# Two graph layers: weight bursts of seven pairs, the turned u of layer 1 on ScalarE, and numerators set apart

## The chip, the cores and the metric

The kernel runs on one core of one Trainium2 chip. The metric is the device time in microseconds; lower is better. A kernel's time is the median of several executions. One execution is recorded by the hardware profiler, and all durations below come from that one.

## The reference

Two graph layers, each with a residual and a layer norm, on x of 8 batches, 2048 nodes and 64 features, with a dense adjacency matrix A of 2048 x 2048:

```python
def layernorm(x): ...                       # over the 64 features

# layer 0: supports I, A, 2AA - I
x_g = einsum('knm,bmc->bnkc', [I, A, 2*A@A - I], x)
w   = einsum('nd,dkio->nkio', embedding, weight)      # weights of every node, d = 16
x   = layernorm(x + einsum('bnki,nkio->bno', x_g, w) + embedding @ bias)

# layer 1: supports I, A, 2AA - I, softmax(relu(E @ E.T))
apt = softmax(relu(E @ E.T), axis=1)
x_g = einsum('knm,bmc->bknc', [I, A, 2*A@A - I, apt], x)
w   = einsum('nd,dkio->nkio', E, weights_pool)
x   = layernorm(x + einsum('bnki,nkio->bno', x_g, w) + E @ bias_pool)
```

All is in float32. Every node has weights of its own, made from its 16-number embedding.

## The kernel before, in words

The nodes are cut into 8 blocks of 256 (j). The work is 40 stages, one after the other: A0 (u = A x, layer 0), B0 (A u), A1 (u = A x, layer 1), Z1 (softmax times x), V1 (A u), each for j = 0 to 7; stage n is 8 times the phase plus j. `A0` and `A1` are the "u stages". Most stages form their product by Strassen's seven half-size products (`strassen`, `times`): seven accumulations of 8 steps, 56 steps in all. A step in A0 and A1 is one matmul of 128 x 128 by 128 x 256, which the profile lists as two rows. The other stages have 64 steps.

Around the steps of a product the rest of the work is laid by hand. `put(n, place, job)` books a job in stage n at a place from 0 to 64; a stage of 56 steps scales it by 56/64. `catch_up` runs after each step whatever is due. All engines keep the program's order (`Pinned`), so the booking is the order of the work on every engine and in every queue.

The jobs that matter here are these.

- `weights` (line 327) makes the weights of the block's 256 nodes: 32 pairs of matmuls (the two of a pair stand in rows 0 to 63 and 64 to 127 of the array), tile name `pw`, from a slice of the weight tensor (`wst`) and the repeated embeddings (`e2`). Before, the unit is a group of two pairs, four matmuls, in one `ps_big` tile of two PSUM banks: each row half has a bank of its own. Three groups are made in a burst, since there are three such tiles; a stage has 16 groups in bursts of 3, 3, 3, 3, 2, 2. Each group is read out to `w` by ScalarE, some by VectorE, as 128 x 1024.
- The weights of stage n are made in stage n + 1, where also its `turn` (the transposes `pt` of u), its `apply` (64 matmuls `po`, 128 rows of the profile) and `post` stand.
- `wst` is an `Ahead` queue of three tiles of eight pairs each. A stage needs four slices, 0 to 3, loaded by SP's DMA queue (512 KB each). A tile is loaded again once the matmuls that read it are over. Before, the queue is filled when the next slice is taken, and at the end of a stage.
- `adj`, another such queue of four tiles on SP's DMA queue, brings the pieces of A or their sums, one for each of the seven products.
- The accumulators `ps_acc` are two single banks used in turn, one for each of the seven products; the three `ps_big` tiles have the other six banks.
- `store_c` stores the softmax's row maxima and inverse sums (`cd`) by POOL's queue, in each A1 stage; `store_u` stores u of A1 by SP's.
- `numerators` and `normalize` make the softmax's numerators for stage 25 in stage 24, on PE, VectorE and ScalarE.

The loading queue, as it was:

```python
def next(self):
    self.fill()
    return self.ready.pop(0)
```

Of the kernel before, what the change touches and what calls it, by code (L numbers as in the profile page):

```python
# [9 lines left out]
F32 = mybir.dt.float32  # L10
F32R = mybir.dt.float32r
AF = mybir.ActivationFunctionType
# [3 lines left out]
P = 128  # L16
N = 2048
B = 8
C = 64
D = 16  # L20
NJ = N // P
BC = B * C
NB = 256
# [6 lines left out]
V1 = C // 4  # L30
# [18 lines left out]
def two_graph_layers(ctx: ExitStack, tc: tile.TileContext, x, x_t, adj_b, adj_q, layers, out):  # L49
# [30 lines left out]
    three = ctx.enter_context(tc.tile_pool(name="three", bufs=3))  # L80
    small = ctx.enter_context(tc.tile_pool(name="small", bufs=2))
    dram = ctx.enter_context(tc.tile_pool(name="dram", bufs=1, space=bass.MemoryType.DRAM))
    ps_acc = ctx.enter_context(tc.tile_pool(name="ps_acc", bufs=2, space=PSUM))
    ps_big = ctx.enter_context(tc.tile_pool(name="ps_big", bufs=3, space=PSUM))

    def heads(t):
        return t.rearrange("p (b c) -> p b c", b=B)

    def big(name):
        return ps_big.tile([P, 2, 512], F32, tag="big", name=name)  # L90

    def copy(i, dst, src):

        if i % 2:
            act.activation(dst, src, AF.Copy)
        else:
            dve.tensor_copy(dst, src)
# [42 lines left out]
    ps = big("pi")  # L140
# [87 lines left out]
    class Ahead:  # L228
# [10 lines left out]
                self.load(t, self.order.pop(0))  # L239
                self.ready.append(t)  # L240

        def next(self):
            self.fill()
            return self.ready.pop(0)

    def load_adj(t, key):
# [26 lines left out]
    class Stage:  # L273
# [50 lines left out]
                pool.dma_start(out=rows, in_=heads(bx))  # L324


        def weights(self, g0, g1):
            if g0 == 0:
                self.w = w_room[:, 0:NB * self.units].rearrange("p (n o) -> p n o", n=NB)
            made = []  # L330
            for g in range(g0, g1):
                if g % 4 == 0:
                    self.ws = wst.next()
                ps = big("pw").rearrange("p h (v n) -> p h v n", n=NB)
                for i in range(2):
                    for h in range(2):
                        r = slice(64 * h, 64 * h + 64)
                        pe.matmul(ps[:, h, i, :], self.ws[r, 2 * (g % 4) + i, :], self.e2[r, :],
                                  start=True, stop=True)
                made.append(ps)  # L340
            if g1 == self.units // 4:
                wst.fill()
            for g, ps in zip(range(g0, g1), made):
                dst = self.w[:, :, 4 * g:4 * g + 4].rearrange("p n (v h) -> p n v h", h=2)
                copy(0 if self.n and g % (8 if self.phase == "A0" else 3) == (2 if self.phase == "A0" else 1) else 1, dst, ps.rearrange("p h v n -> p n v h"))


        def apply(self, c):
# [65 lines left out]
        def turn(self, k, feature=None):  # L414
            slabs = X[SB * self.j:SB * self.j + SB] if feature == "x" else self.slabs
            order = list(range(SB) if feature == "x" or self.phase == "A0" else reversed(range(SB)))
            ps = big("pt")
            psv = ps.rearrange("p a (q n) -> p (a q) n", n=P)
            for s in order:
                for q in range(BQ):  # L420
                    pe.transpose(psv[:, s * BQ + q, :], slabs[s][:, q * P:(q + 1) * P], ident)
            t = self.features()
            for s in order:
                for par in range(2):
                    src = psv[64 * par:64 * par + 64, s * BQ:(s + 1) * BQ, :]
                    copy(s, t[64 * k:64 * k + 64, s * P:(s + 1) * P, par::2], src.rearrange("p q n -> p n q"))


        def product(self):
# [26 lines left out]
                yield [a[:, i, :] for i in range(4)]  # L456

        def accumulator(self, name):
            return ps_acc.tile([P, BC], F32, tag="acc", name=name)

        def straight(self, right):
            accs = [self.accumulator("pu") for _ in range(SB)]
# [331 lines left out]
    def put(n, i, f, *args):  # L794
        plans[n].setdefault(i * stages[n].length / 64, []).append((f, args))

    def spread(n, first, last, jobs):
        for i, job in enumerate(jobs):
            put(n, first + (last - first) * i / max(len(jobs) - 1, 1), *job)
# [25 lines left out]
        put(32, place, sums["V1"].make, i)  # L825
    for n, st in enumerate(stages):
        phase = st.phase
        cuts = (0, 3, 6, 9, 12, 14, 16) if st.units == C else (0, 3, 6, 8)
        if phase == "V1" and st.j:
            put(n, 4, st.weights, 0, 1)  # L830
            cuts = (1, 4, 7, 10, 13, 16)
        weights = [(st.weights, *g) for g in zip(cuts, cuts[1:])]
        bursts = None
        if phase == "A0":
            for c in range(NJ // 4 if st.j == 1 else 0):
                put(n, 16 * c + 10, st.sums_of_a, c)
            spread(n + 1, 1, 31, weights)
            turned, bursts, posts = 33, (38, 38, 38, 38), (50,)
        elif phase == "B0":
            for c in range(NJ // 4 if st.j == 0 else 0):  # L840
                put(n, (10, 26, 36, 57)[c], st.sums_of_a, c)
            if st.j == 7:
                spread(n, 35, 54, weights)
                bursts, posts = (0, 0, 6, 10), ()
                put(n + 1, 16, st.load_x, range(SB))
                for k in range(6):
                    put(n + 1, (11 if k < 3 else 12.5) + 0.5 * k, st.post, k % 3, 8 - k // 3 * 8, 16 - k // 3 * 8)
            else:
                spread(n + 1, 3, 13, weights)
                bursts, posts = (19, 19, 29, 29), (38, 46.5, 50)  # L850
                put(n + 2, 5, st.load_x, range(SB))
        elif phase == "A1":
            spread(n + 1, 12, 34.5, weights)
            turned, bursts, posts = 4, (43, 43, 43, 43), (56,)
            for s, h, place in ((0, 0, 38), (0, 1, 40), (1, 0, 57), (1, 1, 60)):
                put(*((n, place) if st.j or s == 0 else (n + 1, place - 43)), st.scores_of_rows, s, h)
            put(n, 41, st.statistics, 0)
            put(*((n, 62) if st.j else (n + 1, 19)), st.statistics, 1)
            put(n + 1, 24, st.store_c)
        elif phase == "V1":  # L860
            spread(n, (22 if 0 < st.j < 7 else 12 if st.j else 4), (62 if st.j < 7 else 42), weights)
            bursts, posts = (4, 4, 4, 4), (15, 19, 23)
            put(n, 20, st.load_z)
        if bursts and n + 1 < len(stages):
            if phase[0] == "A":
                put(n + 1, turned, st.turn, 1)
            for i, place in enumerate(bursts):
                put(n + 1, place, st.apply, i if phase == "A0" else i ^ 2)
            for k, place in enumerate(posts):
                put(n + 1, place, st.post, k)  # L870
        if n + 1 < len(stages):
            if n < 24 or n > 30:
                put(n, 44 if n < 23 else 37 if n < 24 else 4, stages[n + 1].load_e)
        if phase[0] == "A":
            put(n, 48 if n == 0 else 36 if st.li == 0 else 38.5, st.bias)
            if st.li == 0:
                put(max(n, 1), 20 if n else 4, st.load_xt)
            else:
                put(n, 47 if st.j else 57, st.turn, 0, "x")
        if phase != "Z1":  # L880
            put(*((1, 26) if n == 0 else (n, 54) if st.kk == 0 else (n, 30)), st.load_acc)
        elif st.narrow:
            put(24, 1, st.take_halves)
            put(23, 48, st.load_e)
            for t, places in enumerate(((3, 5, 37), (7, 10, 40))):
                for i, place in enumerate(places):
                    put(24, place, *((st.numerators, t, i) if i < 2 else (st.normalize, t)))
            put(26, 10, load_last_phase)
        elif st.wide:
            first, even, odd = (n - 2, (16, 24, 32), (40, 48, 56)) if n % 2 == 0 else (n - 2, (28, 36, 44), (4, 12, 20))  # L890
            load = ((25, 40) if n == 28 else (n - 3, 4)) if n % 2 == 0 else (n - 3, 10)
            if n == 26:
                first, even, odd, load = 25, (4, 12, 18), (22, 30, 36), (24, 40)
            elif n == 27:
                first, even, odd, load = 25, (66, 69, 72), (44, 52, 58), (25, 8)
            put(*load, st.load_e)
            for t, places in enumerate((even, odd)):
                for i, place in enumerate(places):
                    at = (first, place) if place < 64 else (first + 1, place - 64)
                    put(*at, *((st.numerators, t, i) if i < 2 else (st.normalize, t)))  # L900
        else:
            st.p = [None] * 8
            for c in range(8):
                if c < 3:
                    put(n - 1, (50, 54, 62)[c], st.scores, c)
                else:
                    put(n, 8 * (c - 2), st.scores, c)
# [73 lines left out]
```

## Time and profile before

| What | Value |
|---|---|
| median of 3 runs | 1468.82 us (1468.38 to 1470.13) |
| profiled execution | 1470.19 us |
| its span, first to last instruction | 1468.3 us |
| TensorE busy | 1440.8 us, 98% of the span |
| VectorE busy | 973.9 us, 66% |
| ScalarE busy | 478.3 us, 33% |
| GpSimd busy | 204.6 us, 14% |
| matmuls `pw` | 1728 (wst) and 64 (first stage), 146.5 and 5.3 us busy |
| read-outs of `pw` | 330 on ScalarE at 1.02 us, 118 on VectorE at 1.22 us |
| loads of `wst` | 108 of 512 KB, median 6.1 us from issue to landing |
| granted TensorE clock | 0.998 of full speed |

Busy is the time in which an engine has an instruction at work, and instructions of one engine can overlap. The profile's groups give, after a bar, the idle time of the engine just before the group's instructions and what ended it. The chain of waits is followed back from the last instruction, and shows at each place what the end hung on. In the timelines and the chain the first number is the start in us, the second the duration, and "x12" the count of rows merged.

### The profile page before, as it was taken

The numbers are of one execution on the slowest core, as the hardware profiler recorded it, in microseconds if no ns is written. First come the engines' busy times: TensorE is split into PE (matmuls) and PEld (weight loads), VectorE is DVE, ScalarE is ACT, GpSimd is POOL, SyncE is SP. The second block draws the span as 40 slices with busy tenths as digits, with TensorE's granted clock in tenths as the row PEclk, the third lists the DMA queues.
The fourth block names the chain that finished last, engine by engine and source line by source line (L and its number), as shares of the span: only waits on it lengthen the run. The fifth ranks groups of instructions, "written<-read, shape, count | busy, mean of one in ns | idle before, by whom it ended". The sixth has DMA issues, their size and how long they took to land.

```text
span 1468.3 us, 31599 instructions
## 1 busy us (share of the span) xinstructions
PE 1440.8 (98%) x13502; PEld 1184.9 (81%) x13502; DVE 973.9 (66%) x1655; ACT 478.3 (33%) x597; POOL 204.6 (14%) x339
## 2 busy tenths in 40 slices
PE   9999999999999999999999999999999999999996
PEld 4577777778999999567777777799888988888885
DVE  3866666648676766865666666679794666666666
ACT  0444444432211213154444344612110233333332
POOL 4212221110111111211011111011000000000000
PEclk9999999999999999999999999999999999999999
DMA  9888888886666666578887977223313766666662
GB/s 361 274 262 276 282 280 265 281 313 190 209 192 201 205 201 206 157 177 180 205 201 162 207 205 186 35 73 101 90 44 105 236 196 190 189 194 191 190 206 59
DMA packets 88380, 285.50 MB, mean 194 GB/s; under 512 B 14000, under 2 KB 19632, under 8 KB 86640
## 3 DMA queue, kind: packets, MB, share of 16 engines
q1 hardware_dynamic: 55568, 175.13, 41.0%
q0 software_dynamic: 27200, 94.71, 21.4%
q10 hardware_dynamic: 5472, 13.63, 2.8%
q8 instruction: 107, 1.75, 0.5%
q14 instruction: 33, 0.27, 0.1%
HBM read 217.33 MB, written 62.41 MB: 191 GB/s over the span
## 4 chain that ended last, share of the span: by engine, by line
PE 91%; DVE 4%; DMA 3%; ACT 1%; issue 1%; ACTq 0%; DVEq 0%
PE p L43 58%; PE po L43 14%; PE pw L43 9%; PE pu L43 4%; PE pz L43 4%; DMA wst<-wd 2%; PE pt L43 1%; PE pr L43 1%; PE ps L43 1%; DVE acc L43 1%; DMA x<-in_x 1%; DVE u L43 1%; DVE t L43 0%; DVE p L43 0%; ACT t L43 0%
## 5 line engine op out<-in xcount | busy, mean ns | idle before, releaser
L43 ACT ACTIVATE w<-pw 128x1024 f32<-128x1024 f32 x330 | 320.1, 1021 | 444.4 <-PE pw L43 442.6
L43 DVE SCALAR_TENSOR_TENSOR acc<-po,mask,acc 128x256 f32<-128x256 f32 (+1 forms) x640 | 247.1, 426 | 66.8 <-PE po L43 56.5
L43 DVE COPY w<-pw 128x1024 f32<-128x1024 f32 x118 | 144.4, 1224 | 142.3 <-PE pw L43 142.1
L43 PE MATMUL p<-a,u 128*128 128x128 f32 x1920 | 234.1, 278 | 0.6 <-issue 0.6
L43 PEld LDWEIGHTS p<-a,u 128*128 128x128 f32 x1920 | 221.2, 192 | 8.8 <-issue 2.4
L43 PE MATMUL po<-w,t 128*32 128x256 f32 (+1 forms) x5120 | 206.9, 337 | 7.0 <-issue 5.8
L43 PE MATMUL p<-u,a 128*128 128x256 f32 x832 | 204.3, 388 | 0.0
L43 PEld LDWEIGHTS po<-w,t 128*32 128x32 f32 (+1 forms) x5120 | 128.3, 108 | 79.3 <-issue 16.3
L43 PEld LDWEIGHTS p<-u,a 128*128 128x128 f32 x832 | 151.6, 190 | 29.2 <-issue 5.4
L43 PE MATMUL p<-x,a 128*128 128x256 f32 x624 | 152.4, 384 | 0.0
L43 PE MATMUL pw<-e,wst 64*128 64x256 f32 x1728 | 146.5, 297 | 4.3 <-DMA wst<-wd 2.5
L43 PEld LDWEIGHTS pw<-e,wst 64*128 64x128 f32 x1728 | 112.5, 184 | 46.0 <-issue 23.9
L43 PEld LDWEIGHTS p<-x,a 128*128 128x128 f32 x624 | 114.7, 190 | 19.3 <-issue 0.5
L43 PE MATMUL p<-a,x 128*128 128x128 f32 x768 | 93.0, 277 | 0.0
L43 PEld LDWEIGHTS p<-a,x 128*128 128x128 f32 x768 | 88.3, 192 | 2.5 <-PE pw L43 0.2
L43 PE MATMUL pu<-x,a 128*128 128x512 f32 x192 | 87.0, 600 | 2.1 <-DMA x<-in_x 2.1
L43 PE MATMUL p<-w,u 128*128 128x256 f32 x384 | 85.8, 379 | 0.0
L43 PE MATMUL p<-a,w 128*128 128x128 f32 x672 | 81.3, 277 | 0.0
L43 PEld LDWEIGHTS p<-w,u 128*128 128x128 f32 x384 | 72.0, 190 | 9.3
L43 PEld LDWEIGHTS p<-a,w 128*128 128x128 f32 x672 | 77.3, 192 | 2.5 <-issue 1.4
L43 PEld LDWEIGHTS pu<-x,a 128*128 128x128 f32 x192 | 35.1, 190 | 42.7 <-issue 37.1
L43 DVE TENSOR_TENSOR temps<-p,temps 128x256 f32<-128x256 f32 x115 | 45.8, 420 | 34.1 <-PE p L43 33.3
(129 smaller groups left out, 1372.7 us busy)
## 6 DMA issues: line engine op xcount, KB each, us to landing
wst<-wd SPq DMA_DIRECT2D x108, 512.0 KB, 6.1
a<-in_adj_q SPq DMA_DIRECT2D x90, 512.0 KB, 5.3
a<-sd SPq DMA_DIRECT2D x88, 512.0 KB, 4.6
sd<-a POOLq DMA_DIRECT2D x24, 512.0 KB, 6.3
bx<-bx POOLq DMA_DIRECT2D x32, 256.0 KB, 5.9
acc<-bx POOLq DMA_DIRECT2D x16, 512.0 KB, 7.1
pd<-acc POOLq DMA_DIRECT2D x16, 512.0 KB, 5.3
acc<-pd POOLq DMA_DIRECT2D x16, 512.0 KB, 8.7
```

Of the source, the lines that this page charges most:

```text
L43: return self._tc.keep_in_program_order(f(*args, **kwargs))
```

## The change

Twelve stage products (n = 1 to 6 and 17 to 22, so A0 and A1 with j = 1 to 6) have their weights made in bursts of 4, 7, 7, 7 and 7 pairs, where there were six bursts of 6, 6, 6, 6, 4 and 4. Six pairs of a burst of seven stand in the three big tiles as before. The seventh, the last by number, stands in the accumulator bank that is not in use. As both of its row halves then write to one bank, they are put at the two ends of the burst: the half in the lower rows is the burst's first matmul, that in the upper rows its last. A one-element activation on ScalarE ("seen") reads the first one's result, and the last matmul waits for it. The spare bank is read out by ScalarE as 128 x 512, after the first big tile.

The places of these bursts are listed by hand. The weight queue is filled after each burst, not ahead of taking a slice, and counts the slice still in use. Which groups VectorE reads out is chosen anew. In layer 1, the copies out of the turned u are all ScalarE's, where VectorE had half. For stage 25 the numerators of the second half and both normalizations change places.

The diff's core:

```diff
-    ps_acc = ctx.enter_context(tc.tile_pool(name="ps_acc", bufs=2, space=PSUM))
+    ps_acc = ctx.enter_context(tc.tile_pool(name="ps_acc", bufs=1, space=PSUM))
...
+    in_use = [0]
+    in_turn = mybir.DependencyInfo(mybir.DependencyClass.Sync, mybir.DependencyReason.DATA)
+
+    def acc_bank(i):
+
+        return ps_acc.tile([P, BC], F32, tag=f"acc{in_use[0] ^ i}", name="pa")
...
-        def next(self):
-            self.fill()
+        def next(self, fill=True):
+            if fill or not self.ready:
+                self.fill()
             return self.ready.pop(0)
...
-        def weights(self, g0, g1):
-            if g0 == 0:
+
+        def weights(self, v0, v1):
+            if v0 == 0:
                 self.w = w_room[:, 0:NB * self.units].rearrange("p (n o) -> p n o", n=NB)
...
+                self.ws = {}
+            for c in range(v0 // 8, (v1 - 1) // 8 + 1):
+                if c not in self.ws:
+                    self.ws[c] = wst.next(fill=False)
+            pairs = list(range(v0, v1))
+            made = [(v, big("pw").rearrange("p h (v n) -> p h v n", n=NB)) for v in pairs[:-1:2]]
+            spare = []
+            if len(pairs) % 2:
+                spare = [pairs.pop()]
+                made.append((spare[0], acc_bank(1).rearrange("p (h v n) -> p h v n", h=2, n=NB)))
+            for at in zip(spare + pairs, pairs + spare):
+                for h, v in enumerate(at):
+                    r = slice(64 * h, 64 * h + 64)
+                    i, ps = (v - v0) % 2, made[(v - v0) // 2][1]
+                    ins = pe.matmul(ps[:, h, i, :], self.ws[v // 8][r, v % 8, :], self.e2[r, :], start=True, stop=True)
+
+                    if v in spare and not h:
+                        seen = act.activation(small.tile([1, 1], F32, tag="seen", name="seen"), ps[0:1, h, i, 0:1], AF.Copy)
+                    elif v in spare:
+                        tc.add_manual_dep(ins.ins, seen.ins.name, in_turn, reason="one bank, two row tiles")
+            wst.held = 1 if v1 % 8 else 0
+            wst.fill()
+            if spare:
+                made.insert(1, made.pop())
+            for k, (v, ps) in enumerate(made):
+                m = 1 if v in spare else 2
+                dst = self.w[:, :, 2 * v:2 * v + 2 * m].rearrange("p n (v h) -> p n v h", h=2)
+                on_dve = k == (0 if self.phase == "V1" else len(made) // 2) and v not in spare and self.n and (v > 16 if self.phase == "A0" else self.phase != "V1" or v0)
+                copy(0 if on_dve else 1, dst, ps.rearrange("p h v n -> p n v h"))
...
-                    copy(s, t[64 * k:64 * k + 64, s * P:(s + 1) * P, par::2], src.rearrange("p q n -> p n q"))
+                    copy(1 if self.phase == "A1" and feature is None else s, t[64 * k:64 * k + 64, s * P:(s + 1) * P, par::2], src.rearrange("p q n -> p n q"))
...
-            return ps_acc.tile([P, BC], F32, tag="acc", name=name)
+            in_use[0] ^= 1
+            return acc_bank(0)
...
+        sevens = n in (*range(1, 7), *range(17, 23))
+        cuts = (0, 2, 8, 14, 20, 26, 32) if phase == "V1" and st.j else (0, 6, 12, 16) if st.half else (0, 4, 11, 18, 25, 32) if sevens else (0, 6, 12, 18, 24, 28, 32)
         weights = [(st.weights, *g) for g in zip(cuts, cuts[1:])]
...
         if phase == "A0":
...
-            spread(n + 1, 1, 31, weights)
-            turned, bursts, posts = 33, (38, 38, 38, 38), (50,)
+            if sevens:
+                place_weights(n + 1, (1, 5, 14, 23, 32))
+                turned, bursts, posts = 34.5, (39.5, 39.5, 39.5, 39.5), (51,)
+            else:
+                spread(n + 1, 1, 31, weights)
+                turned, bursts, posts = 33, (38, 38, 38, 38), (50,)
...
         elif phase == "A1":
-            spread(n + 1, 12, 34.5, weights)
+            if sevens:
+                place_weights(n + 1, (1, 12.5, 17, 22.3, 31.3))
+            else:
+                spread(n + 1, 12, 34.5, weights)
...
-            for t, places in enumerate(((3, 5, 37), (7, 10, 40))):
+            for t, places in enumerate(((3, 7, 22), (37, 39.5, 57))):
```

More of the change, by code (lines that the diff above doesn't have):

```diff
@@ L324, in bias @@
                 pool.dma_start(out=rows, in_=heads(bx))
-        def weights(self, g0, g1):
-            if g0 == 0:
+        def weights(self, v0, v1):
+            if v0 == 0:
                 self.w = w_room[:, 0:NB * self.units].rearrange("p (n o) -> p n o", n=NB)
[L330 to L345, printed above, removed]
+                self.ws = {}
[26 more added lines that the diff above has]
+                copy(0 if on_dve else 1, dst, ps.rearrange("p h v n -> p n v h"))
@@ L827, in two_graph_layers, with place_weights @@
         phase = st.phase
[L828 to L831, printed above, removed]
+        sevens = n in (*range(1, 7), *range(17, 23))
+        cuts = (0, 2, 8, 14, 20, 26, 32) if phase == "V1" and st.j else (0, 6, 12, 16) if st.half else (0, 4, 11, 18, 25, 32) if sevens else (0, 6, 12, 18, 24, 28, 32)
         weights = [(st.weights, *g) for g in zip(cuts, cuts[1:])]
+        def place_weights(n, places):
+            for place, job in zip(places, weights):
+                put(n, place, *job)
         bursts = None
@@ L860, in two_graph_layers @@
         elif phase == "V1":
+            if st.j:
+                put(n, 4, *weights.pop(0))
             spread(n, (22 if 0 < st.j < 7 else 12 if st.j else 4), (62 if st.j < 7 else 42), weights)
```

## The prediction

> **What bounds the kernel now.** I read the page's busy times first.
>
> ```profile
> PE 1440.8 (98%) x13502; PEld 1184.9 (81%) x13502; DVE 973.9 (66%) x1655; ACT 478.3 (33%) x597; POOL 204.6 (14%) x339
> ```
>
> TensorE (PE) is busy in all but 27.5 us of the 1468.3 us span. So a change pays only by shortening PE's own work, and costs what it makes PE wait. ScalarE has room on average. The groups by shape show the weight matmuls and their waits:
>
> ```profile
> L43 PE MATMUL pw<-e,wst 64*128 64x256 f32 x1728 | 146.5, 297 | 4.3 <-DMA wst<-wd 2.5 <-DVE p L43 0.7 <-DVE sq L43 0.5
> L43 ACT ACTIVATE w<-pw 128x1024 f32<-128x1024 f32 x330 | 320.1, 1021 | 444.4 <-PE pw L43 442.6
> ```
>
> To price a burst I took PE's timeline of one stage A0 (start us, us, instruction, count):
>
> ```profile
> 116.62 0.97 PE L43 MATMUL pw<-e,wst 64*128 64x256 f32 x12
> 117.53 2.86 PE L43 MATMUL p<-x,a 128*128 128x256 f32 x12
> 120.31 0.97 PE L43 MATMUL pw<-e,wst 64*128 64x256 f32 x12
> ...
> 130.09 0.74 PE L43 MATMUL pw<-e,wst 64*128 64x256 f32 x8
> 130.76 0.92 PE L43 MATMUL p<-u,a 128*128 128x256 f32 x3
> ```
>
> Start to start, a burst of 12 takes 0.91 us and one of 8 takes 0.67: 0.06 each and 0.19 fixed. The 12 product matmuls after the first burst take 2.78 us; undisturbed ones take 6.14/28 = 0.219 us each (a run of 28 from 106.50 to 112.64), or 2.63. That is 0.15 more. **A burst costs 0.34 us whatever its size.** A step of the product is two such rows, 0.438 us.
>
> Then the chain of waits in one stage A1, which starts at 752.55 (first burst less 11 steps and 0.87 us of transposes, 5.69 us):
>
> ```profile
> 758.31 0.91 PE pw L43 x12
> 759.22 1.92 PE p L43 x8
> 761.14 0.48 PE pw L43 x5
> 761.62 8.57 DMA wst<-wd
> 770.19 0.14 issue
> 770.32 0.74 PE pw L43 x8
> ```
>
> This is the line that decides. The stage's last slice of weights (wst, slice 3) is asked for when burst 2 frees a buffer (761.62) and lands 8.57 us later, just when burst 5 needs it (PE waits 0.68 us). The other A1 stages are alike: issued 9.06 us after the stage's start, landed 17.18, 16.41, 17.64, 17.76, not recorded, and 17.77 us after it. It is late not because it is asked for late. The same stretch of the next-earlier stage (starting at 711.17), by windows (us, busy ..., PEclk, DMA share, GB/s):
>
> ```profile
> 714.00:723.00 9.00, 9.00 (x62) 7.14 (x62) 3.83 (x4) 5.98 (x10) 0.00 (x0) 1.00 0.64 60
> 723.00:728.00 5.00, 5.00 (x38) 3.94 (x34) 3.21 (x6) 3.88 (x4) 0.72 (x1) 1.00 1.02 357
> ```
>
> For 9 us the DMA engines report themselves 64% busy and move 60 GB/s; then the backlog drains at 357. Each of the sixteen small stores cd (1 KB each, two per A1 stage, one issued at 711.86) is followed by such a stretch. Ahead of slice 3 on SP's queue stand the stores of u (0.5 MB) and two loads of adjacency (1 MB), so it comes out after them.
>
> **What the Trainium skill says.** TensorEngine Tiling (Key Properties): changing the tiling mode drains the TensorE. The trace agrees; the 0.34 us are that price. The same page (Gotcha 1: PSUM Pressure): different row tiles cannot access one PSUM bank at once. The trace before shows no such pair, as each half has its own bank; the change needs a handshake for it. DMA: Bandwidth & Descriptors (Queues, rings and completion order): on each engine descriptors are consumed in ring order. The landings agree: adjacency issued at 754.39 and 757.05 landed at 766.38 and 767.65, the slice of 761.62 after them. TensorE: Matmul & The Clock Gate (What's actually happening): an idle window of about 3.4 us halves the clock. PE's longest gap inside the work here is 1.34 us, so only the kernel's end shows it (0.72 of the clock at 1460 to 1464 us).
>
> **The change part by part.**
>
> *Bursts of seven.* Twelve stage products (six A0, six A1) have five bursts, of 8, 14, 14, 14, 14 matmuls, for six. The matmul count stays. A0: 6 x 0.34 = -2.0 us. A1: also -2.0.
>
> *The handshake.* The spare pair's first matmul is followed by a one-element read on ScalarE ("seen"), and the burst's last matmul waits for it. A matmul lasts 0.28, ScalarE starts 0.09 after a finished group (as at 717.41), and the ScalarE rows of 512 and 256 elements (0.60, 0.375) extrapolate to 0.16 for one: 0.6 us, against 13 x 0.06 = 0.8 until the last matmul. Nothing, if ScalarE is free. In A0 it has per burst at most 0.2 + 3 x 0.96 + 0.55 + 0.39 (a product's copy) = 4.0 us between bursts 4.7 apart; so it is, narrowly. The spare is read out second and needed three steps (1.3 us) after the burst; I find some 0.2 us to spare. Bounds 0 and 0.5 us for each of A0's two tightest bursts, 0 to 6 us; I take +0.5. A0's slice 3 is needed 8.7 us after its issue; there it lands in 4.5 to 5.3 us. No wait.
>
> *The earlier need in A1.* The seventh pair of burst 4 is pair 24, of slice 3, and its matmul is the burst's first. Burst 4 stands at step 20: 20 x 0.438 + 0.87 (transposes) + 0.82 (burst of 8) + 2 x 1.18 (bursts of 14) = **12.8 us after the stage's start**, against 17.0 for burst 5 before. The load is issued at about 6.7 us instead of 9.06, yet behind the same stores, loads and slow stretch; the small store that starts the latter hangs on the end of the preceding stage, which the change leaves. So it lands where it did, at 16.4 to 17.8. Waits: 4.4, 3.6, 4.8, 5.0, 4.1 (the landing not recorded taken as 16.9) and 5.0 = 26.8 us. The waits of before, 2.5, are in that. Net **+24.3**; with the bursts saved, A1 gives +22.3. Behind the waiting matmul stands all of PE's order. An earlier issue could gain at most its own 2.4 us; I take 0.
>
> *Turned u on ScalarE, A1 alone.* Sixteen copies leave VectorE (0.69 us each) for ScalarE (0.64). At a stage's start ScalarE then has two exponentials and their reads (to 2.9 us), one eviction (0.96), four copies (2.5) and a product's copy (0.37): done at 6.9, while burst 2 wants that product's bank at 6.5. A wait of 0.45; burst 3 ends one step before a product that takes the bank of its spare, another 0.7. Both lie ahead of slice 3's landing, which swallows them: 0. Without that cover they cost 6 x 1.2 = 7 us.
>
> *Numerators apart.* In stage 24 (Z1, j=0) PE waits 1.34 us (scores) and 0.75 us (weights) behind VectorE, whose queue holds both halves' numerators and the turned u at once. The second half moves to places 37, 39.5 and 57, and the copies go: -2.1. Bounds -2.1 and +1, if three score tiles in a row held up the apply matmuls at place 43.
>
> *The rest.* Weight loads filled after each burst, three more VectorE evictions (121 for 118), other pairs chosen for them, and banks by name: SP's order shifts only by a slice ahead of an adjacency load, with no wait where PE stands. Zero, cover: PE's weight queue three tiles deep; -1 to +2.
>
> Sum: -2.0 + 0.5 + 22.3 - 2.1 = +18.7 us. The profiled execution took 1470.19 us (span 1468.3 and 1.9 around it), 1.37 above the median of the runs, 1468.82. So 1488.9 as profiled, **1487.5** as a median.
>
> **The rivals.**
>
> *The slice comes in time* (faster). Weight loads have a median of 6.1 us to landing; issued at 6.7 us, slice 3 would then be there at 12.8, just at burst 4. This decides if the slow stretch is not bound to the small stores but to what PE or the evictions do, and moves with them. Then A1 gives -2.0 - 2.5 and up to +7 of ScalarE's waits, and the total is between -8.1 and -0.9; at the middle 1464.3. Against it: sixteen small stores, sixteen slow stretches, and other stages, with the same evictions, load in 4.5 to 6.
>
> *The wait also costs clock.* Gaps of 3.6 to 5.0 us reach the skill's window. If each brings one window of 3.4 us at half speed, 1.7 us is lost in six stages, 10 us more: 1497.7. For it the length; against it that the window runs free and may not fit into so short a gap.
>
> *The bursts save nothing* because the shared bank stalls each one: 24 A0 bursts with up to 0.3 us give +7 for the +0.5, 1494. ScalarE's margin there is thin.
>
> **How the numbers follow.** About 0.2%, 2.9 us, is what a measurement of this kernel can tell from no change. Forecast 0.72, clock lost 0.09, banks stalling 0.06: all slower; the slice in time 0.13, split 0.10 faster and 0.03 within. The forecast's own range is 1480 (an earlier issue gaining 1 us a stage) to 1491. The low end lies a little below that, the high end takes in most of the clock case: 1474 to 1497.
>
> **What would show it.** In the changed kernel: PE's wait for DMA wst rises from 2.5 us to about 27, in six gaps some 42 to 46 us apart in A1, each before the first matmul of burst 4; the A0 period shrinks from 38.7 to about 38.4; the two waits of stage 24 are gone; PE's busy time falls by about 4 us. I am wrong if slice 3 lands under 13 us after its stage's start, if A1's stages don't grow by 3 to 5 us, or if PE waits for "seen" in A0.

## The result, and the profile after

The change makes the kernel slower by 22.0 us: 1490.63 us (median of 4 runs, 1488.82 to 1493.45) against 1468.60 before (the three runs above and a fourth), ratio 1.0151 with a 95% interval of 1.0139 to 1.0163. The prediction said 1487.5, in a range of 1474 to 1497. The profiled execution took 1490.48 us, its span is 1488.6, which is 20.3 us more than the span before: the profiled execution before was 1.6 us slower than the median. The terms below are read from the profiles, so they add up to 20.3.

The page after, its busy times and the chain by line:

```profile
PE 1441.8 (97%) x13502; PEld 1187.5 (80%) x13502; DVE 967.1 (65%) x1642; ACT 496.4 (33%) x682; POOL 204.1 (14%) x339
...
PE pa L43 65%; PE po L43 13%; PE pw L43 7%; DMA wst<-wd 4%; PE pt L43 1%; DVE acc L43 1%; PE ps L43 1%; PE pr L43 1%; DMA x<-in_x 1%; DVE u L43 1%; DMA a<-in_adj_q 0%; DVE mean L43 0%; DMA sd<-sums 0%; ACT w L43 0%; DVE w L43 0%
```

PE is busy for almost the same time (1441.8 against 1440.8 us); the span has grown around it. Accumulators are now named pa, and so are the two matmuls of a burst's spare pair, which write to the same banks. What PE waited for (us in total, times, longest):

```profile
PE pa L43 <- DMA wst<-wd: 15.1, 6, 4.0
...
PE pa L43 <- ACT w L43: 3.4, 6, 0.6
PE pa L43 <- ACT temps L43: 2.7, 6, 0.5
...
PE pa L43 <- ACT seen L43: 0.3, 1, 0.3
```

Three waits, six times each: the slice of weights, and two of ScalarE's. The handshake ("seen") shows once, at 0.3 us. The six are the A1 stages with bursts of seven; the chain of waits in one of them, which starts at 757.7 (the stage starts are worked out from the first apply matmul ahead of them, to some 0.1 us):

```profile
764.38 0.38 ACT temps L43
764.76 0.04 issue
764.80 0.38 PE pa L43
765.18 0.48 PE pw L43 x10
765.66 8.30 DMA wst<-wd
773.96 0.14 issue
774.10 0.35 PE pa L43
```

First ScalarE's copy of a product, which burst 2 waits for; then slice 3, asked for 8.0 us after the stage's start and landed 16.3 after it; then, at once, burst 4's first matmul. The same stretch by windows (us, busy PE, PEld, DVE, ACT, POOL, then PEclk, DMA share, GB/s):

```profile
766.00:769.00 3.00, 3.00 (x23) 2.38 (x23) 1.28 (x2) 2.66 (x5) 0.00 (x0) 1.00 0.51 35
769.00:774.20 5.20, 2.54 (x12) 1.61 (x12) 0.84 (x1) 2.14 (x4) 0.00 (x0) 1.00 0.97 375
```

The slow stretch of before is still there, 35 GB/s, and the queue then drains at 375 with PE idle for half of the time. In A0 the bursts themselves take what was forecast. PE's timeline:

```profile
119.05 0.39 PE L43 MATMUL pa<-e,wst 64*128 64x256 f32 x1
119.06 1.09 PE L43 MATMUL pw<-e,wst 64*128 64x256 f32 x12
119.87 0.27 PE L43 MATMUL pa<-e,wst 64*128 64x256 f32 x1
120.08 1.56 PE L43 MATMUL pa<-x,a 128*128 128x256 f32 x6
```

Fourteen matmuls take 1.03 us (119.05 to 120.08), as 0.19 + 14 x 0.06 says. An A0 stage takes 38.24 us, before 38.72.

By phases, from the first apply matmul of one stage to that of the next: A0 -2.1 us (272.0 for 274.1), B0 +0.8, the six A1 stages +22.8 (273.9 for 251.1), stage 24 -1.55 (47.40 for 48.95), Z1 +0.1, V1 +0.7; the kernel's start -0.5.

### The profile page after: what moved, and what is told of

Its sections match the earlier page's. It is cut to its first block, busy times and chain, and to the rows that moved or that the text cites. A ratio compares the mean times of both kernels' runs of the same rounds, so it can differ in the third digit from the quotient of the medians.

```text
span 1488.6 us, 31613 instructions
## 1 busy us (share of the span) xinstructions
PE 1441.8 (97%) x13502; PEld 1187.5 (80%) x13502; DVE 967.1 (65%) x1642; ACT 496.4 (33%) x682; POOL 204.1 (14%) x339
## 4 chain that ended last, share of the span: by engine, by line
PE 89%; DMA 5%; DVE 4%; issue 1%; ACT 1%; ACTq 0%; SPq 0%; DVEq 0%
PE pa L43 65%; PE po L43 13%; PE pw L43 7%; DMA wst<-wd 4%; PE pt L43 1%; DVE acc L43 1%; PE ps L43 1%; PE pr L43 1%; DMA x<-in_x 1%; DVE u L43 1%; DMA a<-in_adj_q 0%; DVE mean L43 0%; DMA sd<-sums 0%; ACT w L43 0%; DVE w L43 0%
## 5 line engine op out<-in xcount | busy, mean ns | idle before, releaser
L43 PE MATMUL pa<-a,u 128*128 128x128 f32 (+1 forms) x2048 | 264.3, 285 | 2.5 <-issue 2.4
L43 PEld LDWEIGHTS pa<-a,u 128*128 128x128 f32 x2048 | 245.0, 192 | 15.2 <-issue 5.2
L43 PE MATMUL pa<-x,a 128*128 128x256 f32 (+1 forms) x816 | 239.2, 435 | 1.2 <-DMA x<-in_x 1.2
L43 PE MATMUL pa<-u,a 128*128 128x256 f32 x832 | 205.4, 391 | 3.4 <-ACT w L43 3.4
L43 PEld LDWEIGHTS pa<-x,a 128*128 128x128 f32 x816 | 149.7, 190 | 61.5 <-issue 37.6
L43 PEld LDWEIGHTS pa<-u,a 128*128 128x128 f32 x832 | 153.8, 192 | 34.5 <-ACT w L43 5.8
L43 PE MATMUL pa<-a,x 128*128 128x128 f32 x768 | 93.0, 277 | 0.0
L43 PEld LDWEIGHTS pa<-a,x 128*128 128x128 f32 x768 | 88.3, 192 | 2.4
L43 PE MATMUL pa<-w,u 128*128 128x256 f32 x384 | 85.8, 379 | 0.0
L43 PE MATMUL pa<-a,w 128*128 128x128 f32 x672 | 81.3, 277 | 0.0
```

Source lines behind the costliest of these rows:

```text
L43: return self._tc.keep_in_program_order(f(*args, **kwargs))
```

## The experiments

Each ratio is to runs of the kernel before that were made beside the experiment. Their median was 1468.84 us beside e1 to e4, 1466.73 beside e5 to e8 and 1466.46 beside e9 and e10, so across these groups the ratios are compared, not the times.

**Take the bursts of seven away, all or in A1 alone.**

```diff
-        sevens = n in (*range(1, 7), *range(17, 23))
+        sevens = False                # e1
+        sevens = n in range(1, 7)     # e2
```

Expected of e1: 

> No stage has bursts of seven; all else of the change stays (fill after each burst, banks by name, turned u on ScalarE, numerators apart, VectorE's choice of groups). Theory 1 (the early need of slice 3 in A1 is the whole loss): A1's waits for wst fall from 15.1 to about 2.5 us as in the kernel before, the two waits of stage 24 are still gone, so about 1.5 us under the kernel before, 1467. Theory 2 (the loss comes from the fill after each burst or the copies on ScalarE): it stays near 1490, or at least 5 us above the kernel before.

Expected of e2: 

> Bursts of seven in layer 0's six u stages alone; layer 1's are six bursts as before. Theory 1: the saved bursts of A0 come on top of the run without any bursts of seven, about 2 to 2.5 us, so 1464.5 to 1465.5, and no wait for wst in A1 over 2.5 us in all. Theory 2 (the shared bank's handshake stalls each burst, and A1 shows it): A0 gains nothing or loses, 1467 or above.

e1: 1467.92 us, ratio 0.9996 (0.9987 to 1.0005). e2: 1468.17, ratio 0.9999 (0.9991 to 1.0008). Both are back at the kernel before, so the loss hangs on A1's bursts of seven. PE's waits for wst are 2.2 and 0.9 us in all. But A0's gain is not seen in e2's time, which is what its theory 2 said, though the profile has the gain (A0 272.05 us) and shows one wait for the handshake, of 0.3 us. Against e1's profile, what takes it back is B0 (321.1 us for 319.8) and stage 24 (48.83 for 47.40). In the nine profiles with bursts of seven in A0, B0 takes 320.1 to 322.0; in the three without, 319.2 to 319.8. Its own instructions are in the same order. That B0 gives back about 1.2 us is measured. By the traces 1.1 us of it are waits of PE for which the profile names no cause: they sum up to 5.6 to 7.6 us in B0 in the nine profiles and to 4.9 to 5.7 in the three. They are of the kind that e7 shows below; why they are longer was not tested.

**Turn the two small stores round.** The inverse sums, which wait for ScalarE, go ahead of the row maxima in POOL's queue, so that both start well after slice 3 is asked for.

```diff
-            for k, a in enumerate((cst, inv[:, :, 0])):
+            for k, a in ((1, inv[:, :, 0]), (0, cst)):
```

Expected in the changed kernel, e3: 

> The changed kernel with one thing turned round: of store_c's two small stores, the inverse sums go ahead of the row maxima in POOL's queue. The first waits for ScalarE until some 14 us into the stage, so the second, too, starts only after slice 3 is needed. Theory 1 (the small store slows the DMA engines): slice 3 lands 4.5 to 6.5 us after its issue, the wait of 15.1 us before burst 4 is gone or under 2 us, and with it the two drops of the clock (3.8 us); ScalarE's waits in A1 (0.46 and 0.56 us a stage) stay. 1490.6 - 15 - 3.8 = about 1472. Theory 2 (the slow stretch belongs to the store of u or to PE's bursts): slice 3 still lands 16.4 to 17.8 us after the stage's start, 1488 to 1492.

e3: 1472.93 us, ratio 1.0032 (1.002 to 1.0045); some 18 us of the 22 are gone. PE no longer waits for wst at all. Slice 3 of the stage that starts at 710.7, asked for at 718.7:

```profile
L43 SPq DMA_DIRECT2D wst<-wd x1: 320/320/320, 718.7 to 718.7; - x1
...
DMA to landing us min/median/max: 3.3/3.3/3.3
```

In the six stages it lands 3.3 to 4.2 us after its issue, 11.3 to 12.2 after the stage's start; in the change 7.7 to 10.2 after the issue, 15.7 to 18.2 after the start. In the stage that starts at 710.7 the two stores are now issued at 727.9 and 728.6. The same columns by windows:

```profile
719.00:727.00 8.00, 7.42 (x51) 5.68 (x52) 3.31 (x4) 6.39 (x11) 0.00 (x0) 1.00 0.61 199
732.00:740.00 8.00, 8.00 (x91) 5.70 (x94) 5.91 (x13) 2.88 (x4) 2.15 (x4) 1.00 0.69 28
740.00:744.00 4.00, 4.00 (x67) 2.42 (x60) 3.79 (x9) 0.36 (x2) 0.00 (x0) 1.00 0.90 358
```

The stores were moved and nothing else, and the slow stretch went with them; one stretch follows both, where each had its own. So the store at the stage's start makes slice 3 late. Why so small a store slows the DMA engines was not tested. ScalarE's waits stay, 6.2 us in all.

Expected in the kernel before, e4: 

> The kernel before with the same turn of the two small stores. Theory 1: its own 2.5 us of waits for slice 3 go, 1466; the stretch of slow DMA then follows both stores, some 14 us into the stage, where loads of the next stage stand that aren't needed for 20 us. Theory 2: no change, 1468.6; or a new wait for adjacency in A1, slower.

e4: 1468.61 us, ratio 0.9996 (0.9988 to 1.0005). In its profile the waits for slice 3 are gone (the six A1 stages take 249.5 us for 251.1), but the runs show no gain: the interval goes from 1.8 us faster to 0.7 slower. A gain of 1.6 us fits it, the forecast one of 2.5 does not.

**Give slice 3 more time.** Bursts 2 to 5 of A1 stand at steps 12, 19, 26 and 29; the stores are as in the change.

```diff
-                place_weights(n + 1, (1, 12.5, 17, 22.3, 31.3))
+                place_weights(n + 1, (1, 13.6, 21.6, 29.6, 33))
```

Expected, e6: 

> The changed kernel with A1's bursts 2 to 5 at steps 12, 19, 26 and 29 in place of 11, 15, 20 and 28; the small stores stand as in the change. Slice 3 is needed at about 15.4 us after the stage's start in place of 12.8. Theory 1 (it lands 16.4 to 17.8 us after the start whatever the schedule): the wait shrinks to 1 to 2.4 us a stage, too short for the clock to drop, so 1472 to 1477. Theory 2 (the landing moves with the bursts, a fixed time after the issue): the waits of 1.5 to 4.0 us stay, 1488 to 1491.

e6: 1468.15 us, ratio 1.0011 (1.0003 to 1.0019), below what was expected. The slice lands 15.2 to 17.1 us after the start, as in the change, needed or not. PE waits 4.4 us in four stages, where it waited 15.1 in six. ScalarE's waits are gone too; burst 2 comes a step later, and no burst is followed by a product's end one step on. So the places of four bursts decide over some 20 of the 22 us.

**ScalarE's part.** To e3's stores, the turned u split between VectorE and ScalarE as before.

```diff
-                    copy(1 if self.phase == "A1" and feature is None else s, t[...], ...)
+                    copy(s, t[...], ...)
```

Expected, e5: 

> The run with the inverse sums stored first, and besides the turned u of layer 1 read out half by VectorE and half by ScalarE again. With the slice in time, ScalarE's two waits in each A1 stage stand free (0.46 us at the first matmul of burst 2, 0.56 us at the product after burst 3). Theory A (the four copies at the stage's start make ScalarE late for burst 2): two copies fewer, 1.26 us, clear the first wait, the second stays; six stages by about 0.5 to 0.7 us, 1469 to 1470. Theory B (both waits come from burst 3 standing one step before a product's end and from the handshake): 1472.9, no change.

e5: 1468.48 us, ratio 1.0015 (1.0008 to 1.0021). The wait of 0.46 us at burst 2 is gone, that of 0.58 after burst 3 stays (3.5 us in all); an A1 stage takes 41.80 us, in e3 42.31. So the four copies make ScalarE late for burst 2. By the ratios e5 is 2.5 us under e3, a little less than the 3 to 4 expected. Stage 24 takes 48.64 us with split copies, 47.40 with ScalarE's: of the 1.55 us gained there, 1.2 come from the copies and 0.3 from the numerators. (The other profiles agree, but for e2's, where stage 24 has ScalarE's copies, another wait of 1.19 us for ScalarE, and takes 48.83, and e10's, below.)

**Put together.** e7 has bursts of seven in A0 alone and e3's stores.

Expected, e7: 

> Bursts of seven in layer 0 alone, and the inverse sums stored first. Theory 1: the saved bursts (2.1 us), the waits for slice 3 (up to 2.5 us) and most of the waits of stage 24 add up, less about 1 us that B0 gives back, 1463 to 1465.

e7: 1472.19 us, ratio 1.0041 (1.0028 to 1.0054); its six runs lie between 1468.70 and 1476.95. A plain miss. In the profiled execution one A1 stage takes 48.58 us in place of 41.4. PE's timeline in it:

```profile
859.66 5.14 PE L43 MATMUL po<-w,t 128*32 128x256 f32 x90
869.99 3.72 PE L43 MATMUL po<-w,t 128*32 128x256 f32 x34 [5.19 <-issue]
```

PE stops for 5.19 us amid the apply matmuls, and the trace names no instruction and no load that it waited for. The clock is then at half for 3.41 us. The trace's packets do show one thing: a packet of 16 KB of the queue named "instruction" lands 1.44 us before PE goes on. In all twelve profiles every PE wait of this kind between 360 and 1100 us, 0.24 to 5.19 us long, ends 1.2 to 1.6 us after such a packet, of which a kernel has 107. Those near 58 and 1180 us do not. With both small stores one after the other the slow stretch lasts from 853 to beyond 860 and stands ahead of the apply matmuls. That PE runs out of instructions because their packets are held up too is the reading that fits; it was not tried by itself. e3, with its stores in the same order, has one such stop in A1, of 1.79 us.

e8 has bursts of seven in both layers, e6's places, e3's stores and e5's copies.

Expected, e8: 

> Bursts of seven in both layers, with A1's at the late places, the inverse sums stored first and the turned u split between VectorE and ScalarE. Theory 1: nothing is late in A1 any more, so that its six bursts saved show at last, about 0.5 us each: 3 us under the run with A0 alone, 1460 to 1462. Theory 2 (a burst of seven in A1 costs what it saves, by ScalarE's read-outs and the shared bank): not under 1464.

e8: 1465.51 us, ratio 0.9992 (0.9984 to 1.0). Nothing in A1 waits for a slice or for ScalarE; five of the six stages take 41.15 us against 41.38 (one has a stop of 0.69 us). So a burst saved in A1 is worth 0.23 us and not 0.5: theory 2 is nearer. From start to start, the matmuls of the bursts take hardly less (4.91 us in a stage of e9 with 41.25 us, 4.97 before), and those of the product 24.50 for 24.58.

e9 is e8 with the copies all on ScalarE.

Expected, e9: 

> As the run with late places and the inverse sums first, but with all of the turned u of layer 1 read out by ScalarE, as in the change. With burst 2 at step 12, some 6.9 us into the stage, ScalarE is just done with the four copies and the product's copy, so that no wait comes back in A1; in stage 24, where the runs with split copies took 48.6 us and those with ScalarE's 47.4, 1.2 us go. So 1.2 us less than that run, ratio to the kernel before 0.998 to 0.9985. If ScalarE is late after all, 0.3 us and more in each of six stages, and no gain.

e9: 1464.88 us, ratio 0.9989 (0.9982 to 0.9995), short of the expected 0.998 to 0.9985. It is the best version here, faster than the kernel before by 1.6 us; that is less than the 0.2% that I called measurable, but the interval leaves out 1. Stage 24 is back at 47.39 us, and nothing in A1 waits for ScalarE. The runs don't tell e9 from e8.

e10 moves both small stores to place 45, behind the apply matmuls.

```diff
-            put(n + 1, 24, st.store_c)
+            put(n + 1, 45, st.store_c)
```

Expected, e10: 

> The same, with the two small stores moved to place 45 of the stage, some 29 us into it, behind the apply matmuls. Theory: the slow stretch of the DMA engines also holds the 16 KB packets of the queue named instruction, and PE, short of instructions, stopped 0.7 to 5.2 us in the apply matmuls when the stretch fell ahead of them. Then no such stop stands in the apply matmuls of A1, and the slice, needed at 15.4 us of the next stage, is still in time unless the stretch lasts 16 us: equal to the run beside it or up to 1 us faster. If the stretch runs into the next stage's start, waits for wst come back, up to 2 us a stage, and it is slower by up to 10 us.

e10: 1479.88 us, ratio 1.0086 (1.0072 to 1.01), slower than feared. PE's waits:

```profile
PE pa L43 <- DMA wst<-wd: 7.0, 6, 1.6
PE ps L43 <- DMA e<-ed: 5.9, 1, 5.9
```

No stop stands in A1's apply matmuls, as expected (a weak test, as e9 beside it has but one, of 0.34 us), but the slow stretch reaches into the next stage's start: slice 3 is late again in all six stages, and in stage 24 the load of the embeddings, which comes after the stores in POOL's queue, is 5.9 us late; the clock is at half for 6.8 us there. The stores hurt whatever needs a transfer soon after them.

## Why the prediction was right, and where its terms were off

- *The early need of slice 3*, the deciding step, is shown: the landing stays about where it was (15.7 to 18.2 us after the start, before 16.4 to 17.8), and a need forecast at 12.8 us in place of 17.0 became a wait. e3 takes away what makes it late, e6 the early need; each takes most of the loss away.
- *Its size.* Forecast: 26.8 us of waits, with ScalarE's swallowed. Measured: 15.1 for the slice and 6.1 for ScalarE, 21.2 in all. The waits for ScalarE lie ahead and are swallowed indeed: they shorten the slice's. The 5.6 us too many have two sources. In the stage that starts at 757.7, burst 4 starts 16.4 us in; without its three waits (0.46, 0.56 and 2.10 us) it would stand at 13.3, not 12.8. And the landings are on average some 0.5 us earlier than those that were taken from the kernel before. The load was issued at 8.0 us, not 6.7: burst 2 waited 0.46 us and stood later than reckoned.
- *The clock*, which I gave 9% as a rival, came in two of six stages. PE's timeline at the first:

```profile
820.04 0.35 PE L43 MATMUL pa<-e,wst 64*128 64x256 f32 x1 [2.27 <-DMA wst<-wd]
820.04 1.43 PE L43 MATMUL pw<-e,wst 64*128 64x256 f32 x12
821.10 0.41 PE L43 MATMUL pa<-e,wst 64*128 64x256 f32 x1
821.45 3.20 PE L43 MATMUL pa<-u,a 128*128 128x256 f32 x8
```

  Eight rows take 3.0 us there (to 824.48), elsewhere 1.9: the records show half speed for 3.41 us from 820.51, and again from 912.67, 1.7 us lost each time.
- *A1 as a whole, and luck.* 12.6 us more for the slice (15.1 less 2.5), 6.1 for ScalarE, 3.4 for the clock and one stop of 0.9 in the apply matmuls are 23.0; measured 22.8, which leaves 0.2 for the six bursts saved, where e9 and e8 give 0.8 to 1.4. Forecast for A1 was 22.3. That this is so near is luck: waits forecast 5.6 us too long are made up for by the clock (3.4), the stop (0.9) and bursts that saved 1.8 us less than reckoned.
- *The bursts saved.* A0: forecast 0.34 us a stage, measured 0.48 in five of the six; the first saves nothing. There the one wait for the handshake stands, 0.3 us long, and that burst takes 1.70 us in place of 1.03. In all A0 gains 2.1 us, forecast 1.5 (2.0 less 0.5 for the handshake). A1: forecast 0.34, measured 0.13 (e9) to 0.23 (e8). The price was taken from A0's timeline, and it does not carry over to A1, where the order around the bursts is another. So how much of it is the change of tiling mode, as the prediction says, stays open.
- *Stage 24.* Forecast -2.1, measured -1.55: the wait behind the scores is gone, but one of 0.96 us behind VectorE stands where 0.75 stood.
- *The rest*, taken as zero, is +1.1 (B0 +0.8, V1 +0.7, Z1 +0.1, the start -0.5), within its bounds.
- *The signs named ahead.* PE's busy time did not fall by 4 us but rose by 1.0, as the half clock added 3.4 and the bursts saved less. "PE waits for seen in A0" was a sign of being wrong; it came once, at 0.3 us. The slice landing under 13 us did not come, and A1's stages grew by 2.5 to 6.7 us.

The rival on the other side, that the slice comes in time, did not happen; e3 brings about its condition, a landing 11.3 us after the start. The prediction's sum for it, 0.9 to 8.1 us faster, was too good: e3 is 4.1 us slower than the kernel before. In e3's profile A1 takes 5.0 us more than before: 6.2 for ScalarE and a stop of 1.8, less 2.5 for the slice, which leaves some 0.5 for the six bursts. The rival that the shared bank stalls each burst is out, with one wait in 48.

## What to carry to other kernels

Before a burst is made larger, look for the first use of each operand in it: one pair more moved a load's deadline by nearly 4 us in each of six stages, which cost about ten times what the saved bursts gave. Such a load may be late neither by its issue nor by its own queue but by a small store in another engine's queue, so compare landings with the stage's start too, not with the issue alone. Here two stores of 1 KB in a stage set when the loads landed; where they stand in the order was worth more than the bursts.

## What the runs showed of the hardware

- In the A1 stages a store of 1 KB, or two in a row, is followed by 7 to 9 us in which the DMA engines move 28 to 60 GB/s; in the profiles of before, after and e3 the backlog then drains at 357 to 411. Moving the stores moves the stretch (e3, e10).
- The Trainium skill (TensorE: Matmul & The Clock Gate, What's actually happening) puts the idle window that halves the clock at about 3.4 us. Here a gap of 2.27 us, shorter than that, was enough once, as was one of 3.99; gaps of 2.32 and 2.91 us in other stages were not.
- Between 360 and 1100 us, PE's waits without a named cause end 1.2 to 1.6 us after a 16 KB packet of the instruction queue, in all twelve profiles, and in one A1 stage of e7 such a wait grew to 5.19 us. That the packet is what they wait for was not tested.
